# Attention and binary FFN on one core: fp16 halves of q and k taken straight from PSUM, larger pieces in the stores, and a changed use of the PSUM banks

## The chip, the cores and the metric

The kernel runs on one core of one Trainium2 chip. The metric is the device time of one execution in microseconds (us), the median of the runs shown. One further execution was recorded by the hardware profiler; all durations below come from that one. TensorE is PE in the profile (its weight loads PEld), VectorE DVE, ScalarE ACT, GpSimd POOL, SyncE SP. SP only issues DMAs here.

## What is computed

The input x has 16 sequences of 512 rows and 128 features. Each row is normalised once without weights (xn); then two branches read xn, and the output is x plus both:

```
attention:  y = layernorm(xn) * ln_g + ln_b
            q, k, v = y@Wq+bq, y@Wk+bk, y@Wv+bv     16 heads of 8 features
            p = pe@Wp                               pe: a fixed sinusoidal table
            score = (q+u_bias)·k + shift((q+v_bias)·p)    shift: relative positions
            out = softmax(score * 8**-0.5) · v, all heads, @ Wo + bo
FFN:        h = [xn, -xn] @ (+-1 weights k0) * s0;  h = 2 relu(h)      512 wide
            h = h @ (+-1 weights k1) * s1;          h = 2 relu(h)      512 wide
            h = h @ (+-1 weights k2) * s2                              128 wide
```

All inputs are float32, except that the FFN weights are booleans. To use 16-bit matmuls without losing float32 accuracy, the kernel writes a float32 number as a high half and a low half in fp16: hi is the number rounded, lo is the number less hi.

## The kernel before

The work has two stages in one program.

**First stage** (lines 230 to 776). It walks over the 16 sequences. The spine is the FFN: for each sequence `ffn_layer` (L653) does four 128-wide blocks of layer 1 and then four of layer 0 of the next sequence. A block is a group of matmuls (L640) into one PSUM bank, after which ACT writes hi (L617) and DVE writes lo (L618), both from the bank. `ffn_last` (L665) does the third layer into `a_t`, and `ffn_out` (L682) adds it to the residual rows on DVE (L685, L688) and stores them. Into this spine a queue of closures is fed by `more()` (L749), five times a sequence at a fixed rate: `norm` (L308, statistics and scaling on DVE, L318 to L339, with one square root on ACT), `transposed2` (L505, four PE transposes, hi and lo of xn, and the scaled xᵀ that q, k and v use), `project_q` (L543), `project_k` (L563) and `project_v` (L572). When the queue is empty, `more()` issues the stores and the first loads of the second stage (L746).

The projections go through float32 copies: ACT scales and biases the PSUM result into a float32 tile (`scaled`, L522), ACT casts this to hi (L502), and POOL subtracts to get lo (L503), both in `halves_to`:

```
def halves_to(src, hi, lo):
    nc.scalar.copy(hi, src)
    return nc.gpsimd.tensor_tensor(lo, src, hi, ALU.subtract)
```

For q this is done twice: with u_bias for the content scores, and with v_bias for the positions, where two sequences share one tile of 1024 elements a partition. The halves go to scratch tensors in DRAM: each of hi and lo of k, and of q, is stored twice (`K_PARTS`, `Q_PARTS`), since the second stage contracts hi and lo parts stacked over partitions. q for the content is stored as pairs (number, zero) or (zero, number), so the second stage can read two sequences into one block-structured operand; the zeros come from memsets of `qu_b` at the start (L490 to L492). v is stored with one float32 piece of 36 numbers per head and partition.

`ffn_residual` (L658) loads a sequence's x rows once more and adds the output bias on POOL (L662). At the first sequence four are issued at once. `clear_queries` (L494) zeroes pieces of the second stage's query tiles on POOL, one after each `project_k`.

**PSUM.** One pool holds eight banks for the whole kernel: `a_t`, six score tiles `s_t`, and `t_t`. The first stage uses the score tiles and `t_t` as plain banks: three in rotation for the queue's products, four (`F_BANKS`) in rotation for the FFN.

**Second stage** (from L782). For each head 32 units of 16 rows; a unit's scores are matmuls of queries with keys (L797) and with shifted windows of p (L813, L826); DVE takes maxima (L840, L845, L854), PE subtracts them (L859), ACT takes the exponential (L869), and PE multiplies with v (L887). The order on PE, DVE and ACT is written out by hand (`attention_order`); POOL and SP are placed by the framework's planner. In the first stage the planner places all engines, in the program's order as a priority. On the chip every engine's queue runs in order: an instruction that waits holds up all behind it.

Eight units share a block of queries, double-buffered (`load_queries`, L210): 12 DMAs each, four of q for the content (L216) and eight of q for the positions (L220, L224). `load_head` (L196) loads keys (L202), windows and v (L208) for a head, ahead of time. At each head's end `divided` (L939) loads the head's sums (L942) and their reciprocals (L943), multiplies them on POOL (L946) and stores the product (L947).

Of the kernel before, what the change touches and what calls it, by code (L numbers as in the profile page):

```python
# [9 lines left out]
F32 = mybir.dt.float32  # L10
# [10 lines left out]
P = 128  # L21
# [66 lines left out]
def rel_attention_and_binary_ffn(  # L88
# [47 lines left out]
    def scr(name, shape, dt):  # L136
# [4 lines left out]
    qu_scr = scr("qu_scr", [4, DH * H, B, S, 2], F16)  # L141
    qv_scr = scr("qv_scr", [4, DH * H, 5, NL, NC, UL, B], F16)
    k_scr = scr("k_scr", [4, DH * H, B, S], F16)
    p_scr = scr("p_scr", [4, DH * H, 2, WIN + 4], F16)
    pd_scr = scr("pd_scr", [4, DH * H, 2, 2, WIND + 1], F16)
    v_scr = scr("v_scr", [P, H, B, NC * VW], F32)
# [5 lines left out]
    Q_PARTS, K_PARTS = ((0, 2), (1, 3)), ((0, 1), (2, 3))  # L152
# [23 lines left out]
    ps = ctx.enter_context(tc.tile_pool(name="ps", bufs=1, space=bass.MemoryType.PSUM))  # L176
    e_t = [None, early.tile([P, B, NC, NC, 64], F32, tag="e_1", name="e_1")]

    a_t = ps.tile([P, 2, 2 * P], F32, tag="a", name="a_t")

    s_t = [
        [ps.tile([P, 2, NC, 4, B], F32, tag=f"s_{n}_{m}", name=f"s_{n}_{m}") for m in range(2)]
        for n in range(3)
    ]
    t_t = ps.tile([P, 4, 2, P], BF16, tag="t", name="t_t")

    a_flat = a_t.rearrange("p g i -> p (g i)")
    p_banks = [t.rearrange("p c a b r -> p (c a b r)") for ts in s_t for t in ts]
    p_banks.append(t_t.rearrange("p n f i -> p (n f i)").bitcast(F32))
    F_BANKS = (3, 4, 5, 6)  # L190
    t_bank = p_banks[6].rearrange("p (g i) -> p g i", g=2)
# [4 lines left out]
    def load_head(h):  # L196
        m = h % 2
        src = p_scr.rearrange("t (d h) s j -> (t d) h s j", h=H)[:, h]
        src_d = pd_scr.rearrange("t (d h) s n j -> (t d) h s n j", h=H)[:, h]
        for n in range(4):  # L200
            rows_n = slice(32 * n, 32 * n + 32)
            nc.sync.dma_start(  # L202
                k_t[m][rows_n], k_scr.rearrange("t (d h) b j -> (t d) h b j", h=H)[:, h, n::4, :]
            )
            nc.sync.dma_start(win[m][rows_n], src[:, :, 3 - n : 3 - n + WIN])
            r, side = n // 2, n % 2
            nc.sync.dma_start(win_d[m][rows_n], src_d[:, side, :, 1 - r : 1 - r + WIND])
        nc.sync.dma_start(v_t[m], v_scr[:, h].rearrange("p b f -> p (b f)"))  # L208

    def load_queries(h, l):  # L210
        m = l % 2
        qv = qv_scr.rearrange("t (d h) r l a u b -> (t d) h r l (a u b)", h=H)[:, h, :, l]
        qu = qu_scr.rearrange("t (d h) b i m -> (t d) h b (i m)", h=H)[:, h]
        for n in range(4):
            rows_n = slice(32 * n, 32 * n + 32)
            nc.sync.dma_start(  # L216
                qc_t[m][rows_n, :, n // 2].rearrange("p g i m -> p g (i m)"),
                qu[:, n::4, 2 * l * P : 2 * (l + 1) * P],
            )
            nc.sync.dma_start(  # L220
                qp_t[m][rows_n, :, n].rearrange("p s a u b -> p s (a u b)"), qv[:, n : n + 2]
            )
            r, side = n // 2, n % 2
            nc.sync.dma_start(  # L224
                qd_t[m][rows_n, :, r].rearrange("p t a u b -> p t (a u b)"),
                qv[:, r + side : r + side + 3 : 2],
            )


    with ExitStack() as pre:  # L230
        setup = pre.enter_context(tc.tile_pool(name="setup", bufs=1))
        work = pre.enter_context(tc.tile_pool(name="work", bufs=2))
        turns = {}

        def psw(name, banks=(0, 1, 2)):
            turns[banks] = turns.get(banks, 0) + 1
            return p_banks[banks[turns[banks] % len(banks)]]
# [13 lines left out]
        XB = 4  # L251
# [132 lines left out]
        def vectors():  # L384

            for n in range(2):
                nc.gpsimd.tensor_copy(of_feature(rows_d[:, n]), by_feature(rows[:, n]))
            for dst, src in ((wp_d, wp_sb), (wq_d, wq_sb), (wk_d, wk_sb)):
                before = nc.gpsimd.tensor_copy(of_feature(dst), by_feature(src))
            with tc.issue_after(before.ins):  # L390
                clear()
            pt = psw("ptr_rows")
            for n in range(2):
                nc.tensor.transpose(pt[:, 4 * n : 4 * n + 4], rows_d[:, n], ident[:4, :4])
            nc.tensor.transpose(pt[:, 8:10], gb, ident[:2, :2])
            nc.vector.tensor_copy(cols, pt[:, :10])
# [8 lines left out]
        k_mul = pw[:, 1:2]  # L405
        q_mul = sts("q_mul", [P, 1])
# [15 lines left out]
        def powers():  # L422
# [22 lines left out]
            nc.vector.tensor_scalar(q_mul, pw[:, 0:1], scale, None, ALU.mult)  # L445
            nc.vector.tensor_tensor(e_scale, bmax[:, 0:1], bmax[:, 1:2], ALU.mult)
            nc.vector.tensor_scalar(e_scale, e_scale, 2.0 ** -26, None, ALU.mult)
# [7 lines left out]
        def positions():  # L455
            pp = psw("pp")
            nc.tensor.matmul(pp, lhsT=wp_d, rhs=pe_sb, start=True, stop=True)
            p32 = work.tile([P, S], F32, tag="t32", name="p32", bufs=2)
            nc.scalar.activation(p32, pp, AF.Identity, scale=k_mul)
            halves_to(p32, *[t[:, PAD : PAD + S] for t in p_half])  # L460

        def windows():
            for n in range(2):
                for part in K_PARTS[n]:
                    for side, x0, d0 in ((0, PAD, PAD + S - P + 2), (1, 0, PAD - P + 1)):
                        nc.sync.dma_start(p_scr[part, :, side], p_half[n][:, x0 : x0 + WIN + 4])
                        for t in range(2):
                            nc.sync.dma_start(
                                pd_scr[part, :, side, t], p_half[n][:, d0 - 2 * t : d0 - 2 * t + WIND + 1]
                            )  # L470
# [14 lines left out]
        def clear():  # L485
            for t in v_b:
                nc.gpsimd.memset(t, 1.0)
            for t in p_half:
                nc.gpsimd.memset(t, 0.0)
            for ts in qu_b:  # L490
                for t in ts:
                    nc.gpsimd.memset(t, 0.0)  # L492
# [8 lines left out]
        def halves_to(src, hi, lo):  # L501
            nc.scalar.copy(hi, src)  # L502
            return nc.gpsimd.tensor_tensor(lo, src, hi, ALU.subtract)  # L503
# [18 lines left out]
        def scaled(b, n, src, dst):  # L522

            mul = k_mul if n == 2 else q_mul
            if n < 2:
                src = src.rearrange("p (a l m) -> p l a m", a=NC, l=NL)
                dst = dst.rearrange("p (l a m) -> p l a m", l=NL, a=NC)
            nc.scalar.activation(dst, src, AF.Identity, bias=b_cols[:, n : n + 1], scale=mul)

        def t32(b, n):  # L530
            return work.tile([P, S], F32, tag="t32", name=f"t32_{b}_{n}", bufs=2)

        def stored(b, t, dst, parts):
            hv = [work.tile([P, S], F16, tag=f"hv{m}", name=f"hv{m}_{b}", bufs=2) for m in range(2)]
            last = halves_to(t, *hv)
            for m in range(2):
                for part in parts[m]:
                    nc.sync.dma_start(dst[part, :, b, :], hv[m])
            return last

        two = {}

        def project_q(b):  # L543
            pq = psw(f"pq_{b}")
            nc.tensor.matmul(pq, lhsT=wq_d, rhs=x2T[b], start=True, stop=True)
            n = b % 2

            if n == 0:
                two[0] = work.tile([P, S, 2], F32, tag="two", name=f"two_{b}", bufs=1)
            tu = t32(b, 0)  # L550
            scaled(b, 0, pq, tu)
            scaled(b, 1, pq, two[0][:, :, n])
            halves_to(tu, *[t[:, :, n] for t in qu_b[n]])
            for m in range(2):
                for part in Q_PARTS[m]:
                    nc.sync.dma_start(qu_scr[part, :, b], qu_b[n][m])
            if n == 1:
                halves_to(
                    two[0].rearrange("p (q r) n -> p r q n", r=4),
                    *[q[:, :, :, b - 1 : b + 1] for q in qv_all],  # L560
                )

        def project_k(b):  # L563
            pk = psw(f"pk_{b}")
            nc.tensor.matmul(pk, lhsT=wk_d, rhs=x2T[b], start=True, stop=True)
            t = t32(b, 2)
            scaled(b, 2, pk, t)
            last = stored(b, t, k_scr, K_PARTS)
            with tc.issue_after(last.ins):
                clear_queries(b)  # L570

        def project_v(b):  # L572
# [14 lines left out]
            nc.sync.dma_start(v_scr[:, :, b, :], vb.rearrange("p h c w -> p h (c w)"))  # L587
# [21 lines left out]
        acts = {}  # L609
# [4 lines left out]
        def split(src, hi, lo, relu):  # L614

            if relu:
                nc.scalar.activation(hi, src, AF.Relu)  # L617
                nc.vector.scalar_tensor_tensor(lo, src, 0.0, hi, ALU.max, ALU.subtract)  # L618
# [29 lines left out]
        def ffn_split(b, layer, f, ph):  # L648
            part = parts(b, layer + 1, f)
            split(ph, *part, relu=True)  # L650
# [7 lines left out]
        def ffn_residual(b):  # L658
# [3 lines left out]
            nc.gpsimd.tensor_tensor(rows_of, rows_of, bo_sb.unsqueeze(1).to_broadcast([P, NC, D]), ALU.add)  # L662
# [71 lines left out]
        for b in range(B):  # L734
            queue.append(lambda b=b: project_q(b))
# [28 lines left out]
        for b in range(LAST):  # L764
# [6 lines left out]
            for n in range(RB + 1 if b == 0 else 1):  # L771
                if b + n + (RB if b else 0) < B:
                    ffn_residual(b + n + (RB if b else 0))
# [8 lines left out]
    with ExitStack() as att:  # L782
        manual = ExitStack()
# [363 lines left out]
```

## Time and profile before

| what | value |
|---|---|
| median of 3 runs | 1376.68 us (1376.38 to 1377.88) |
| the profiled execution's own time | 1373.51 us |
| its span, first to last instruction | 1371.7 us |
| mean granted TensorE clock | 0.985 |
| busy PE | 1295.0 us (94%) |
| busy DVE | 1137.7 us (83%) |
| busy ACT | 832.6 us (61%) |
| busy POOL | 130.8 us (10%), 115 instructions |
| first score matmul (L797) | 266.5 us after the start |
| DMA traffic | 160.22 MB, of which 58.80 MB by 290 us |

The page gives for each engine the busy tenths in 40 equal slices of the span, some 34 us each. A row of a group reads: line, engine, operation, tiles, shapes, count; durations are given as min/median/max in ns. A row of an order in time reads: start, length, engine, line, operation, and in square brackets the idle time before it with what ended it. PE's ends are modelled, so a PE that is always busy may still have small waits inside.

### The profile page before, as it was taken

The page shows a single profiled execution, that of the slowest core. Times are in us where ns is not written, and L with a number is a line of the kernel's source. Part 1 is how long each engine was busy: PE and PEld are TensorE (multiplying, and loading weights), DVE is VectorE, ACT ScalarE, POOL GpSimd, SP SyncE. Part 2 cuts the span into 40 slices and gives each one's busy share as a digit, 9 for nine tenths or more (in the row PEclk, how much of TensorE's full clock was granted, in tenths as well). Part 3 has the DMA queues.
Part 4 walks back from the last instruction along what each step waited for, and adds up shares of the span by engine and source line. Part 5 has one row for each costly group of instructions (what it writes and reads, how often), then busy time and mean ns, then how long its engine had stood idle before and what let it go on. Part 6 is the DMA issues. An engine that isn't in the chain of part 4 may idle for free. (4 is left out here: it accounts for less than half of the span.)

```text
span 1371.7 us, 55178 instructions
## 1 busy us (share of the span) xinstructions
PE 1295.0 (94%) x23061; PEld 970.3 (71%) x23061; DVE 1137.7 (83%) x2723; ACT 832.6 (61%) x1456; POOL 130.8 (10%) x115
## 2 busy tenths in 40 slices
PE   4988889999999999999999999999999999999966
PEld 2555555577778777777877877778777777777744
DVE  8988754688888888888888888888888888888846
ACT  4566668466666666666666666666666666566630
POOL 4333345010000000000000000000000000000011
PEclk9999999999999999999999999999999999999988
DMA  4587869873232333333333323333333253323288
GB/s 117 171 222 192 191 171 257 242 220 92 76 99 74 94 79 95 95 86 86 93 89 83 94 74 97 83 93 84 95 80 99 75 128 84 95 74 88 68 146 190
DMA packets 243606, 160.22 MB, mean 117 GB/s; under 512 B 79510, under 2 KB 227100, under 8 KB 243356
## 3 DMA queue, kind: packets, MB, share of 16 engines
q1 hardware_dynamic: 243356, 156.69, 43.5%
q8 instruction: 181, 2.97, 0.9%
q14 instruction: 69, 0.57, 0.1%
HBM read 96.34 MB, written 59.48 MB: 114 GB/s over the span
## 5 line engine op out<-in xcount | busy, mean ns | idle before, releaser
L869 ACT ACTIVATE e<-s,e_scale 128x512 f32<-128x512 f32 x1024 | 623.7, 690 | 218.2 <-PE s L859 218.1
L845 DVE TENSOR_TENSOR m<-s,m 128x256 bf16<-128x256 f32 x1024 | 431.6, 422 | 112.9 <-PE s L826 77.6
L797 PE MATMUL s<-q,k 128*128 128x64 f16 x8192 | 406.7, 193 | 2.1 <-issue 1.0
L859 PE MATMUL s<-ident_b,nm 128*128 128x256 bf16 x2048 | 383.8, 275 | 7.3 <-DVE nm L854 7.3
L797 PEld LDWEIGHTS <-k 128*128 128x128 f16 x8192 | 358.5, 98 | 23.6 <-issue 2.8
L840 DVE TENSOR_REDUCE m<-s 128x256 bf16<-128x512 f32 x512 | 348.2, 680 | 1.0 <-ACT e L869 0.6
L813 PE MATMUL s<-q,win 128*128 128x128 f16 (+1 forms) x4096 | 342.8, 206 | 0.1
L887 PE MATMUL a_t<-e,v 128*9 128x256 f32 x4032 | 266.0, 381 | 0.6 <-ACT e L869 0.6
L813 PEld LDWEIGHTS <-win 128*128 128x128 f16 x4096 | 231.4, 98 | 0.3 <-issue 0.3
L826 PE MATMUL s<-q,win_d 128*128 128x64 f16 x2048 | 227.7, 193 | 0.0
L854 DVE TENSOR_REDUCE nm<-t_t 128x2 bf16<-128x256 bf16 x512 | 214.7, 419 | 7.1 <-PE t_t L850 2.9
L859 PEld LDWEIGHTS <-nm 128*128 128x128 bf16 x2048 | 131.0, 98 | 117.8 <-DVE m L845 99.0
L896 ACT COPY av<-a_t 128x256 f32<-128x256 f32 x126 | 46.9, 372 | 186.2 <-PE a_t L887 161.2
L887 PEld LDWEIGHTS a_t<-e,v 128*9 128x9 f32 x4032 | 86.4, 90 | 81.2 <-issue 1.6
L850 PE MATMUL t_t<-ident_b,m 128*128 128x128 bf16 x1024 | 141.3, 220 | 1.4 <-DVE m L845 1.3
L826 PEld LDWEIGHTS <-win_d 128*128 128x128 f16 x2048 | 129.8, 98 | 0.0
L946 POOL TENSOR_TENSOR raw<-raw,rden 128x512 f32<-128x512 f32 x15 | 19.1, 1273 | 992.3 <-DMA rden<-rden_scr 992.3
L640 PEld LDWEIGHTS <-e 128*128 128x128 f16 x512 | 49.6, 98 | 59.7 <-issue 12.6
L850 PEld LDWEIGHTS <-m 128*128 128x128 bf16 x1024 | 80.9, 98 | 11.3 <-DVE m L845 4.9
L618 DVE SCALAR_TENSOR_TENSOR h2l<-s,h2h 128x512 f16<-128x512 f32 x45 | 30.9, 686 | 37.6 <-ACT h2h L617 37.4
L640 PE MATMUL s<-h1l,e 128*128 128x512 f16 x180 | 47.2, 379 | 0.5 <-DVE h1l L618 0.4
L640 PE MATMUL s<-h1h,e 128*128 128x512 f16 x180 | 47.2, 384 | 0.3 <-DVE h1l L618 0.2
(176 smaller groups left out, 888.3 us busy)
## 6 DMA issues: line engine op xcount, KB each, us to landing
q<-qv_scr SPq DMA_DIRECT2D x512, 64.0 KB
q<-qu_scr SPq DMA_DIRECT2D x256, 64.0 KB
qu_scr<-k SPq DMA_DIRECT2D x32, 256.0 KB
k_scr<-hv SPq DMA_DIRECT2D x64, 128.0 KB
qu_scr<-win SPq DMA_DIRECT2D x32, 256.0 KB
qv_scr<-e SPq DMA_DIRECT2D x16, 512.0 KB
k<-k_scr SPq DMA_DIRECT2D x64, 128.0 KB
win<-p_scr SPq DMA_DIRECT2D x64, 79.5 KB
```

Of the source, the lines that this page charges most:

```text
L640: nc.tensor.matmul(ph, lhsT=w[:, t, f * P : (f + 1) * P], rhs=h[t][m], start=(m == 0 and t == 0), stop=(m == 1 and t == n - 1),)
L797: nc.tensor.matmul(sp[:, c % 2, :, :, 4 * g : 4 * g + 4].rearrange("p a r (n m) -> p n (a r) m", m=2), lhsT=kt[:, g, c * P : (c + 1) * P], ...
L813: nc.tensor.matmul(blocks[:, x0 : x0 + (NC + 1) * (len(cs) - 1) + 1 : NC + 1], lhsT=win[h % 2][:, side, y0 : y0 + P], rhs=qp[:, side, :, c ...
L826: nc.tensor.matmul(blocks[:, x0 : x0 + NC + 2 : NC + 1, 2 * t : 2 * t + 2], lhsT=win_d[h % 2][:, t, UP_OFF - 4 * u : WIND - 4 * u], rhs=qd ...
L840: nc.vector.tensor_reduce(st["m"], flat(st["ps"][0]).rearrange("p c x -> p x c"), AX.X, ALU.max)
L845: nc.vector.tensor_tensor(st["m"], flat(st["ps"][1])[:, c], st["m"], ALU.max)
L850: nc.tensor.transpose(st["pt"][:, f, :], st["m"][:, f * P : (f + 1) * P], ident_b)
L854: nc.vector.tensor_reduce(st["nm"], st["pt"], AX.X, ALU.max, negate=True)
L859: nc.tensor.matmul(flat(st["ps"][half])[:, :, f * P : (f + 1) * P], lhsT=st["nm"][:, f : f + 1].to_broadcast([P, P]), rhs=ident_b.unsqueez ...
L869: nc.scalar.activation(st["eT"][:, :, cs, :, i0 : i0 + 4].rearrange("p b c a r -> p (c a) b r"), st["ps"][half].rearrange("p c a r b -> p ...
L887: nc.tensor.matmul(bank[32 * r : 32 * r + VW, g], lhsT=v_t[h % 2][:, v0 : v0 + VW], rhs=pair["eT"][:, b, c], start=(c == 0 and (g == 0 or ...
L896: nc.scalar.copy(pair[half][:, g], bank[:, g])
```

## The change

- `project_q` takes two sequences at a time into two dedicated banks (`q_banks`). `halves_to` is new: ACT writes hi with the bias from PSUM, DVE writes lo from PSUM (`scalar_tensor_tensor`: PSUM plus bias less hi). The four residues of the position queries are four DVE instructions. The float32 copies `t32` and `two`, and `scaled`, are gone. So is POOL's part.
- `k_mul` and `q_mul` go into the weights (three more DVE operations in `powers`), and the softmax scale into `e_scale`.
- q for the content is stored for two sequences at once as a true pair (half the bytes); on loading, POOL zeroes the number that isn't wanted (four memsets of 32 partitions x 512 elements per `load_queries`). The memsets of `qu_b` are gone.
- hi and lo of k are stored once instead of twice and loaded with two DMAs per group instead of one.
- v is stored in one piece of 2304 bytes a partition and sequence, and loaded per head in pieces of 144 bytes.
- PSUM: `a_t` has a pool of its own; the first stage has `q_banks` (two), two rotating banks for the queue, three for the FFN; the second stage opens its own pool for `s_t` and `t_t` after it.
- Residuals: two at the first sequence, then one a sequence ahead of its use (before: four, then three ahead). `clear_queries` follows the residuals of sequences 2 to 9, two memsets each.
- `XB`, the number of x tiles, goes from 4 to 6; k's halves have three buffers instead of two; the copy of `cols` is issued after the first FFN sequence's splits.

```diff
-    qu_scr = scr("qu_scr", [4, DH * H, B, S, 2], F16)
+    qu_scr = scr("qu_scr", [4, DH * H, B // 2, S, 2], F16)
-    k_scr = scr("k_scr", [4, DH * H, B, S], F16)
+    k_scr = scr("k_scr", [2, DH * H, B, S], F16)
-    v_scr = scr("v_scr", [P, H, B, NC * VW], F32)
+    v_scr = scr("v_scr", [P, B, H, NC * VW], F32)
...
+    Q_PARTS, P_PARTS, K_PARTS = ((0, 3), (1, 2)), ((0, 2), (1, 3)), ((0,), (1,))
...
-            nc.sync.dma_start(
-                k_t[m][rows_n], k_scr.rearrange("t (d h) b j -> (t d) h b j", h=H)[:, h, n::4, :]
-            )
+            for x in range(2):
+                nc.sync.dma_start(
+                    k_t[m][32 * n + 16 * x : 32 * n + 16 * x + 16],
+                    k_scr.rearrange("t (d h) b j -> (t d) h b j", h=H)[:, h, n::4, :],
+                )
...
-        nc.sync.dma_start(v_t[m], v_scr[:, h].rearrange("p b f -> p (b f)"))
+        nc.sync.dma_start(v_t[m].rearrange("p (b f) -> p b f", b=B), v_scr[:, :, h])
...
-                qu[:, n::4, 2 * l * P : 2 * (l + 1) * P],
+                qu[:, n // 2 :: 2, 2 * l * P : 2 * (l + 1) * P],
             )
+            nc.gpsimd.memset(qc_t[m][rows_n, :, n // 2, :, 1 - n % 2], 0.0)
...
+        q_banks = psp.tile([P, 2, S], F32, tag="q", name="q_banks")
+        p_banks = [psp.tile([P, S], F32, tag=f"p_{n}", name=f"p_{n}") for n in range(5)]
+        F_BANKS = (2, 3, 4)
-        def psw(name, banks=(0, 1, 2)):
+        def psw(name, banks=(0, 1)):
...
-            nc.vector.tensor_scalar(q_mul, pw[:, 0:1], scale, None, ALU.mult)
+            for t, mul in ((wp_d, k_mul), (wq_d, q_mul), (wk_d, k_mul)):
+                nc.vector.tensor_scalar(t, t, mul, None, ALU.mult)
...
-            for ts in qu_b:
-                for t in ts:
-                    nc.gpsimd.memset(t, 0.0)
...
-        def halves_to(src, hi, lo):
-            nc.scalar.copy(hi, src)
-            return nc.gpsimd.tensor_tensor(lo, src, hi, ALU.subtract)
+        def halves_to(src, n, hi, lo):
+            nc.scalar.activation(hi, src, AF.Identity, bias=b_cols[:, n : n + 1])
+            for r in range(4) if len(src.shape) == 4 else [slice(None)]:
+                nc.vector.scalar_tensor_tensor(
+                    lo[:, r], src[:, r], b_cols[:, n : n + 1], hi[:, r], ALU.add, ALU.subtract
+                )
...
+            for n in range(2):
+                nc.tensor.matmul(
+                    q_banks[:, n],
+                    lhsT=wq_d,
+                    rhs=x2T[b + n].rearrange("p (a l m) -> p l a m", a=NC, l=NL),
+                    start=True,
+                    stop=True,
+                )
+            qu = qu_b[b // 2 % 2]
+            halves_to(q_banks.rearrange("p n j -> p j n"), 0, *qu)
...
+            halves_to(
+                q_banks.rearrange("p n (q r) -> p r q n", r=4), 1, *[q[:, :, :, b : b + 2] for q in qv_all]
+            )
...
-            nc.gpsimd.tensor_tensor(rows_of, rows_of, bo_sb.unsqueeze(1).to_broadcast([P, NC, D]), ALU.add)
+            last = nc.gpsimd.tensor_tensor(
+                rows_of, rows_of, bo_sb.unsqueeze(1).to_broadcast([P, NC, D]), ALU.add
+            )
+            if 2 <= b < 10:
+                with tc.issue_after(last.ins):
+                    for n in range(2):
+                        clear_queries(2 * (b - 2) + n)
...
-            for n in range(RB + 1 if b == 0 else 1):
-                if b + n + (RB if b else 0) < B:
-                    ffn_residual(b + n + (RB if b else 0))
+            for n in range(2 if b == 0 else 1):
+                if b + n + (1 if b else 0) < B:
+                    ffn_residual(b + n + (1 if b else 0))
```

## The prediction

> **What bounds the kernel now.** I read the slices of the page first, then the busy time by stretch, then the order in time of each engine.
>
> ```profile
> PE   4988889999999999999999999999999999999966
> DVE  8988754688888888888888888888888888888846
> POOL 4333345010000000000000000000000000000011
> ```
>
> There are two stages. Up to slice 8 POOL works and PE is below 9; from 266.5 us on, where the first score matmul (L797) starts, PE is full. The change edits the first stage and the loads of the second.
>
> ```profile
> 40.00:180.00 140.00, 121.79 (x707) 70.83 (x707) 118.09 (x385) 90.83 (x162) 54.11 (x44) 0.95 0.77 201
> 180.00:266.00 86.00, 84.72 (x554) 49.81 (x554) 43.78 (x84) 61.15 (x103) 29.61 (x24) 0.98 0.84 231
> ```
>
> Columns after the length: busy PE, weight load, DVE, ACT, POOL, granted clock, DMA share, GB/s. Where DVE is 84% loaded, PE is 87% busy and the clock 0.95; where DVE is 51% loaded, PE is 98.5% busy. So PE bounds the late part, and DVE keeps PE waiting in the early part. The order in time (115 to 124 us) says how:
>
> ```profile
> 115.03 2.91 POOL L503 TENSOR_TENSOR e<-two,e 128x1024 f16<-128x1024 f32 x1
> 116.46 1.51 DVE L330 TENSOR_TENSOR step<-var,root 128x8 f32<-128x8 f32 x1
> 117.91 1.26 POOL L662 TENSOR_TENSOR sums<-sums,bo_sb 128x512 f32<-128x512 f32 x1
> 118.00 1.20 DVE L331 TENSOR_TENSOR step<-step,root 128x8 f32<-128x8 f32 x1
> 119.14 1.15 POOL L503 TENSOR_TENSOR hv<-t,hv 128x512 f16<-128x512 f32 x1
> 119.23 1.54 DVE L332 TENSOR_SCALAR step<-step 128x8 f32<-128x8 f32 x1
> 124.03 1.01 PE L640 MATMUL s<-sums,w_sb 128*128 128x512 f16 x2 [3.92 <-DVE h2l L618]
> ```
>
> Each eight-column norm step of DVE ends when the POOL instruction above it ends; then PE stands for 3.92 us. These two rows, one of an operation on SBUF alone and one that reads PSUM, tell who is held up:
>
> ```profile
> L332 DVE TENSOR_SCALAR step<-step x16: 164/172/3332, 7.6 to 175.3; 128x8 f32<-128x8 f32 x16
> L618 DVE SCALAR_TENSOR_TENSOR h2l<-s,h2h x45: 654/690/693, 24.1 to 261.9; 128x512 f16<-128x512 f32 x45
> ```
>
> The first stretches from 172 ns to 3332, the second never. Mean less median, times the count, over L335, L332, L685, L325, L330, L331, L326 is 7.7+7.3+6.8+4.4+3.9+3.0+2.6 = 36 us of stalled DVE.
>
> **PE's need in the first stage.** L688 ends an FFN sequence every 10.3 us in the tail (244.7, 255.0, 265.3), where PE is full: 15.3 of them are 158 us. On PE's order in time q, k, v and a transposition take 0.86+0.86+0.88+0.43 = 3.0 us a sequence, 16 times 48; with the set-up, 208. The stage runs from the first FFN matmul, 13.6, to 266.5: 253 us, PE at 82%. The missing 45 are idle gaps (2.92 at 17.5 us, 4.38 at 34, then 19.3 in thirteen gaps, nearly all released by DVE lo halves), slow clock behind them (four 10 us stretches at 0.83 and one at 0.66 are 10 us), and smaller pieces.
>
> **The change, part by part.**
>
> Lo halves from POOL to DVE. POOL loses 16 x 1.156 + 8 x 1.27 + 8 x 1.28 + 8 x 2.90 = 62 us and the 3.66 us memsets of qu_b, in whose shadow L332 stood from 13.34 to 16.67. DVE gains, per pair of sequences: two k halves at 0.69 (L618's shape); one of 1024 elements, 1.13 (from L688's 0.341 at 128 and L618's 0.68 at 512, continued); four of 256, about 0.45 each between the same rows: 4.3, times 8 pairs 34.5 us. They read PSUM, so by L618 POOL can't hold them up. POOL keeps 16 residuals of 1.27 and 16 memsets of 0.52, 29 us; before, 103 busy us of POOL cost 36 of DVE, so 10 remain. DVE has 185 busy us in the stage: 185-36+34.5+10 = 194, against PE's 208. The work is traded, not removed; what goes are the blocks of 1.2 to 3.3 us ahead of the FFN's lo halves. Next late would be DVE in the norm part.
>
> The Trainium skill ("SBUF — State Buffer", Who interferes with whom) says that a DVE instruction with at most one SBUF input and no two-port mode never contends with GpSimd; L618's maximum agrees. It also says that a tensor_tensor with two SBUF inputs contends only with GpSimd reads, so that the 16 memsets would stall tensor_scalars alone; by that the remaining stall would be nearer 7 than 10 us.
>
> ACT loses three scalings (0.777, 0.777, 0.808) and casts from SBUF, and has one pass per half: 69 us become 28. ACT was 65% loaded; this shortens ACT's part of each chain, and I count it with the 90% below.
>
> Residuals: four in a row (27.18, 4.93 us) and a fifth (32.07) stood over the 4.38 gap; now two at first. The clears of q_t follow a residual, so POOL is busy 2.3 us at a time in eight sequences: in the 10 above.
>
> I take PE at 90% of the stage, between the 87% and 98.5% of the two stretches, DVE being 194/231 = 84% loaded without long blocks: 208/0.90 = 231, **22 us saved**. Ends: 82% as now (0), and 96% (36).
>
> PSUM. The FFN has three banks instead of four: layer 0 of a sequence issues four 0.43 us groups at once, and the third now waits for an eviction of 1.3 us, of which 0.86 is covered: 0.45 a sequence, 7 us if always, 0 where queue matmuls stand by; I take 1.5. Two banks for k, v and transposes carry three tiles a sequence instead of four on three; q's own pair is held some 6 us of 28: nothing, unless evictions lag, which is the 82% end. The banks change pools at 266.5: at worst the first scores wait for the last FFN eviction (267.35 + 0.69), 1.5 us; I take 1.
>
> Weights times k_mul, q_mul: three more 128x128 DVE operations (about 0.3 us each, L420) less one of 0.15, once: under 1 us, hidden by FFN matmuls; if not, 1.
>
> Stores: 64 fewer issues of 0.43 us on SP, 12.6 MB of 58.8 less, v in 2304-byte pieces instead of 144. DMA is 77% to 84% busy, but little waits for it (6.7 us, L318): nothing taken.
>
> **Second stage.** PE is full, so only new waits count. Its DVE operations read PSUM and never stretch (L845 361/424/426 beside fifteen L946 of 1.27 us): the 256 POOL memsets cost DVE nothing but for L929 (0.24 us). The weak spot is SP at each head's start:
>
> ```profile
> 577.15 0.60 SPq L931 DMA_DIRECT2D rden_scr<-den  x1
> 578.32 0.45 SPq L207 DMA_DIRECT2D win_d<-pd_scr  x1
> 578.82 0.43 SPq L208 DMA_DIRECT2D v<-v_scr  x1
> 579.57 0.62 SPq L943 DMA_DIRECT2D rden<-rden_scr  x1
> ...
> 586.01 0.34 SPq L947 DMA_DIRECT2D head_scr<-raw  x1
> ...
> 591.03 0.43 SPq L224 DMA_DIRECT2D q<-qv_scr  x1
> ```
>
> SP stands from 581.6 to 586.0 for POOL's multiply, which waits for rden; nine query loads stand behind. The last is issued at 591.46, the first score with it starts at 595.95. This 4.5 us comes back at nearly every head's start, against 8 to 11 at other blocks: these starts wait for the landing. Blocks last 16.15 us, those of head starts 16.2 to 18.8; the excess adds to 11.4 us. Whatever delays rden here delays PE, 15 times.
>
> The v load, just ahead, becomes 2048 pieces of 144 bytes. The trace's DMA records show today's v stores with such pieces spread over 1.9 to 2.2 us when undisturbed, today's v loads over 1.0 to 1.5: +0.7 us. The four more k issues (0.43) a head fall in SP's gaps before; if all came here, +1.7. The memset of the last quarter (0.5 us, as L492's 941 ns for twice the elements) follows a load issued 1.8 us before the last: hidden, if POOL isn't waiting for rden; otherwise up to +0.9. Ends: -11.4 (another order frees the starts) to +50 (3.3 x 15); I take 0.4 x 15 = 6, near the v row, as some starts have slack.
>
> The Trainium skill ("DMA: Bandwidth & Descriptors", Specifications) speaks against this piece: under 512 bytes a transfer falls off line rate. Were 144 bytes as dear as 512 (27 ns in the records against 14), the load would take 3.5 us, +2.3, and 15 starts 34 us: the change would lose. The records of 144-byte stores don't show that; loads of that size no row shows.
>
> **Sum.** The execution profiled took 1373.5 (span 1371.7). -22 +1.5 +1 +6 = -13.5: 1360. The median of the runs is 3.2 higher, 1376.7; so **1363**.
>
> **Rivals.**
> - PE-bound stage (0.20): 96%, and head starts no worse: 36 less 1, 1342 (1334 to 1352). For it: 180 to 266 us. Against: DVE's 194.
> - DVE becomes the bound (0.14): the halves fill what the stalls leave, 40 to 180 us holds 118-26+22+6 = 120 busy us again, and the stage gives 6 to 8 less 5: about 1374 (1371 to 1379). A change that doesn't do what it says ends here too: clears behind residuals stall DVE as the halves did.
> - Slower (0.18): the head-start queue. Rden late by v's small reads and by k issues ahead of it, SP late with nine query loads, PE waiting 15 times. From 19.5/15 = 1.3 us a start it outweighs the first stage; at 2.2 us it gives +13.5, 1390.
>
> The forecast has 0.48 (1352 to 1371). Differences under 0.2% (2.7 us) can't be told from none. Faster: 0.48+0.20+0.08; same 0.06; slower 0.18. The range 1338 to 1382 takes in most of the second case and the near edge of the last.
>
> **What will show it.** L332, L335 and L685 near their medians, and gaps before L640 under 1 us; the clock near 1.0 over 40 to 180; first L797 near 246; DVE above 80% until then. In the second stage: blocks of 16.15 us against the head starts' 16.2 to 18.8, and the gap before head_scr<-raw on SP. I am wrong if L332 still stretches, if PE waits for q's or k's PSUM banks, or if head starts exceed 17.5 us.

## The result, and the profile after

After the change the kernel takes **1437.68 us** (median of 4 runs, 1436.83 to 1438.57); the kernel before, run beside it, 1376.53 (1372.17 to 1377.88). The ratio is 1.0444 [1.0415, 1.0472]: slower, where 1363 (1338 to 1382) was forecast. The profiled execution took 1437.72 us, span 1435.9, mean granted clock 0.959 (before 0.985).

The slices of the page come first, since they show that two opposite things happened:

```profile
PE   6999998999898989898989899989898989898976
DVE  8999765888787878786878787878787868687846
POOL 3111001211111111111111111111111111111111
```

The first slices of PE are fuller than before. But from slice 10 on, where PE read 9 everywhere, almost every other slice is now an 8: one dent for each pair of slices. A slice is 35.9 us and a head lasts about 70, so the dent comes once a head.

The first score matmul moved from 266.5 to 241.4 us: the first stage gained **25 us**. From there to the end it took 1105.2 us before and 1194.5 after: the second stage lost **89 us**.

**First stage.** The stretch from 40 to 180 us, by busy PE, weight load, DVE, ACT, POOL, granted clock, DMA share, GB/s:

```profile
40.00:180.00 140.00, 133.67 (x844) 78.14 (x842) 127.35 (x425) 84.49 (x147) 15.73 (x20) 1.00 0.49 158
```

PE went from 121.79 to 133.67, the clock from 0.95 to 1.00, POOL from 54.11 to 15.73. The norm step that stretched to 3332 ns (L332 before, L330 now) and the FFN's lo halves (L618 before, L596 now), by min/median/max:

```profile
L330 DVE TENSOR_SCALAR step<-step x16: 135/162/529, 7.3 to 144.1; 128x8 f32<-128x8 f32 x16
L596 DVE SCALAR_TENSOR_TENSOR h2l<-p,h2h x60: 669/691/693, 20.4 to 234.8; 128x512 f16<-128x512 f32 x60
```

The step is hardly held any more (529 ns at most); the operation that reads PSUM is as it was. Over all of DVE's groups up to the first score, mean less median, times the count, adds to 38 us before and 15 after.

**Second stage.** The order in time of SP at the end of a head, start and length of each issue:

```profile
573.80 0.62 SPq L938 DMA_DIRECT2D rden<-rden_scr  x1
574.46 0.46 SPq L199 DMA_DIRECT2D win_d<-pd_scr  x1
574.96 0.43 SPq L193 DMA_DIRECT2D k<-k_scr  x1
579.53 0.34 SPq L942 DMA_DIRECT2D head_scr<-raw  x1
579.91 0.43 SPq L193 DMA_DIRECT2D k<-k_scr  x1
580.39 0.43 SPq L197 DMA_DIRECT2D win<-p_scr  x1
580.87 0.43 SPq L199 DMA_DIRECT2D win_d<-pd_scr  x1
581.40 0.56 SPq L200 DMA_DIRECT2D v<-v_scr  x1
582.06 1.37 SPq L208 DMA_DIRECT2D q<-qu_scr  x1
...
589.69 0.42 SPq L217 DMA_DIRECT2D q<-qv_scr  x1
590.22 0.59 SPq L916 DMA_DIRECT2D den<-av  x1
```

As before, SP stands some 4 us (575.4 to 579.5) for POOL's multiply. But now all twelve query loads are behind this, and four pieces of `load_head` between; before, two pieces of it (`win_d`, `v`) and three query loads had been issued ahead and nine were behind. The issue to watch is the last, `den<-av`: it goes out at 590.22, behind everything. This is so at every head: the store goes out ahead of all twelve query loads at 14 of 14 starts (before: at one of 14, and ahead of nine at the others), and `den<-av` goes out 16.6 us after the first score of the block that ends there (median; before: 12.3). DVE and PE at that place:

```profile
587.27 0.68 DVE L835 TENSOR_REDUCE m<-s 128x256 bf16<-128x512 f32 x1
592.09 0.25 DVE L924 RECIPROCAL den<-den 128x16 f32<-128x16 f32 x1 [4.14 <-DMA den<-av]
593.01 0.61 PE L854 MATMUL s<-ident_b,nm 128*128 128x256 bf16 x2 [3.71 <-DVE nm L849]
```

The reciprocal of the sums stands in DVE's order written out by hand, between the maxima of the scores. It waits 4.14 us for a small DMA; every maximum behind it waits too, and PE, which needs the maxima, stands 3.71 us. The same place by stretches (busy PE, clock, DMA share, GB/s) shows a second bill:

```profile
587.00:591.00 4.00, 2.31 (x51) 1.00 0.48 135
591.00:595.00 4.00, 1.99 (x21) 0.60 0.15 28
595.00:599.00 4.00, 4.00 (x59) 0.54 0.34 99
```

PE stands from 589.3 to 593.0. In the second and third stretch the mean granted clock is 0.60 and 0.54: PE starts again slowly, and the block that follows is longer too. Over 300 to 1300 us, the waits of that reciprocal and of PE (total, times, longest), before and then after:

```profile
DVE den L929 <- DMA den<-av: 10.5, 12, 2.6
PE s L859 <- DVE nm L854: 7.2, 9, 2.2
```

```profile
DVE den L924 <- DMA den<-av: 64.8, 13, 7.0
PE s L854 <- DVE nm L849: 59.5, 13, 6.5
```

To sum it up, I took the length of each block of eight units above 16.15 us. The fifteen blocks that end at a head's start exceed it by 10.2 us in all before and by 80.4 after; the fifteen behind them by 2.2 and 17.9; the very first block of the stage lasts 17.4 and 20.2. The differences, 70.2, 15.7 and 2.8, make 88.7 of the 89 us. The 70.2 and 15.7 are the two bills together. PE's standing for the maxima grew by 52 us (7.2 to 59.5). And the trace's record of the clock has 13 stretches at 0.50 between 300 and 1310 us, 6.8 us long but for the first, where before it has none; PE's busy time inside them, halved, is 31 us of lost work (an estimate from this record). Together these are 83 of the 86 us. So more than a third of the loss was paid in clock.

### The profile page after: what moved, and what is told of

It is laid out like the page before. It is cut to its first block, busy times and chain, and to the rows that moved or that the text cites. A ratio compares the mean times of both kernels' runs of the same rounds, so it can differ in the third digit from the quotient of the medians.

```text
span 1435.9 us, 55680 instructions
## 1 busy us (share of the span) xinstructions
PE 1318.8 (92%) x23061; PEld 990.2 (69%) x23061; DVE 1147.0 (80%) x2782; ACT 805.8 (56%) x1399; POOL 236.7 (16%) x326
## 5 line engine op out<-in xcount | busy, mean ns | idle before, releaser
L840 DVE TENSOR_TENSOR m<-s,m 128x256 bf16<-128x256 f32 x1024 | 431.2, 421 | 129.1 <-PE s L821 92.0
L854 PE MATMUL s<-ident_b,nm 128*128 128x256 bf16 x2048 | 397.4, 283 | 64.5 <-DVE nm L849 64.5
L792 PE MATMUL s<-q,k 128*128 128x64 f16 x8192 | 418.3, 196 | 2.3 <-DVE e L596 1.7
L792 PEld LDWEIGHTS <-k 128*128 128x128 f16 x8192 | 372.0, 100 | 27.7 <-issue 3.2
L808 PE MATMUL s<-q,win 128*128 128x128 f16 (+1 forms) x4096 | 350.4, 209 | 0.8 <-issue 0.8
L212 POOL MEMSET q<- 32x512 f16 x256 | 171.7, 671 | 783.6 <-DMA q<-qu_scr 695.4
L808 PEld LDWEIGHTS <-win 128*128 128x128 f16 x4096 | 238.7, 100 | 0.9 <-issue 0.9
L618 PEld LDWEIGHTS <-e 128*128 128x128 f16 x512 | 49.6, 98 | 60.1 <-issue 12.6
L924 DVE RECIPROCAL den<-den 128x16 f32<-128x16 f32 x62 | 15.2, 245 | 84.8 <-DMA den<-av 69.0
L595 ACT ACTIVATE h2h<-p 128x512 f16<-128x512 f32 x60 | 35.9, 598 | 51.5 <-PE p L618 51.3
L618 PE MATMUL p<-h1h,e 128*128 128x512 f16 x240 | 62.7, 382 | 0.0
```

Of the source, the lines that this page charges most:

```text
L212: nc.gpsimd.memset(qc_t[m][rows_n, :, n // 2, :, 1 - n % 2], 0.0)
L618: nc.tensor.matmul(ph, lhsT=w[:, t, f * P : (f + 1) * P], rhs=h[t][m], start=(m == 0 and t == 0), stop=(m == 1 and t == n - 1),)
L792: nc.tensor.matmul(sp[:, c % 2, :, :, 4 * g : 4 * g + 4].rearrange("p a r (n m) -> p n (a r) m", m=2), lhsT=kt[:, g, c * P : (c + 1) * P], ...
L808: nc.tensor.matmul(blocks[:, x0 : x0 + (NC + 1) * (len(cs) - 1) + 1 : NC + 1], lhsT=win[h % 2][:, side, y0 : y0 + P], rhs=qp[:, side, :, c ...
L840: nc.vector.tensor_tensor(st["m"], flat(st["ps"][1])[:, c], st["m"], ALU.max)
L854: nc.tensor.matmul(flat(st["ps"][half])[:, :, f * P : (f + 1) * P], lhsT=st["nm"][:, f : f + 1].to_broadcast([P, P]), rhs=ident_b.unsqueez ...
```

## The experiments

The theory after this comparison: **SP's order**. The second k issue per group (four more a head) makes the planner place `load_head`, the store that waits for POOL, and the queries differently, so `den<-av` goes out late. The rivals: **v's pieces** of 144 bytes delay the chain of `rden`; the **memsets** on POOL delay the multiply, and so the store. For the first stage: **POOL holds DVE**, against fewer passes on ACT. A last group tries to mend the order. "Excess" is that of the fifteen blocks that end at a head's start, "den" the reciprocal's wait over 300 to 1300 us. The median is of all executions; the columns behind the ratio are of the one that was profiled.

| kernel | median us | ratio to before [95%] | first score | rest of the span | first block | excess | den |
|---|---|---|---|---|---|---|---|
| before | 1376.53 |  | 266.5 | 1105.2 | 17.4 | 10.2 | 10.5 |
| after | 1437.68 | 1.0444 [1.0415, 1.0472] | 241.4 | 1194.5 | 20.2 | 80.4 | 64.8 |
| b_k8 | 1432.54 | 1.043 [1.0377, 1.0484] | 269.1 | 1156.4 | 17.4 | 55.5 | 47.5 |
| a_k4 | 1363.97 | 0.9927 [0.9901, 0.9952] | 242.3 | 1122.1 | 21.2 | 23.5 | 22.3 |
| a_poolstore | 1359.91 | 0.9902 [0.9875, 0.9929] | 241.3 | 1116.8 | 22.5 | 15.8 | 14.1 |
| a_early | 1486.68 | 1.0827 [1.0777, 1.0877] | 241.2 | 1240.4 | 21.1 | 0.9 | 0.3 |
| a_early2 | 1360.07 | 0.9891 [0.9861, 0.9921] | 241.2 | 1115.9 | 20.1 | 1.5 | 19.4 |
| a_k4_nomemset | 1359.85 | 0.9891 [0.9861, 0.992] | 239.9 | 1117.4 | 20.0 | 18.3 | 19.0 |
| a_k4_v | 1352.75 | 0.983 [0.9801, 0.9859] | 241.7 | 1111.5 | 21.1 | 10.2 | 7.3 |
| a_k4_pool | 1393.35 | 1.0133 [1.0102, 1.0165] | 266.9 | 1120.8 | 19.7 | 21.5 | 20.3 |
| c_base | 1355.87 | 0.9878 [0.9832, 0.9925] | 240.7 | 1114.2 | 27.5 | 10.3 | 9.1 |
| c_spread | 1359.83 | 0.9911 [0.9873, 0.995] | 242.9 | 1115.1 | 28.2 | 8.8 | 9.4 |
| c_spread_ps | 1351.13 | 0.9835 [0.9799, 0.9872] | 242.4 | 1107.6 | 27.5 | 0.7 | 7.4 |
| c_ps_res2 | 1343.32 | 0.9775 [0.9737, 0.9814] | 241.6 | 1096.1 | 19.1 | 0.8 | 7.8 |

**b_k8** is the kernel before with nothing but k's split load.

```diff
-            nc.sync.dma_start(k_t[m][rows_n], k_scr...[:, h, n::4, :])
+            for x in range(2):
+                nc.sync.dma_start(k_t[m][32*n+16*x : 32*n+16*x+16], k_scr...[16*x : 16*x+16, h, n::4, :])
```

> The kernel before, with one part of the change: each load of keys is split into two loads of 16 partitions (8 issues a head on SP instead of 4, the same bytes). Theory Q (queue order): four more issues a head make the planner put five more of the head's loads, and the store of the divided head that waits for POOL, ahead of all twelve query loads at each head's start; the first stage stays (first score matmul near 266 us) and the second loses what the changed kernel loses, 85 to 90 us: 1460 us. Theory M (the POOL memsets behind the query loads make PE wait) and theory V (the 144-byte pieces of v keep the DMA engines from the queries) both expect no change, 1376 us.

The rest of the span grew by 51 us (85 to 90 were expected), from the same bytes in the same places: four more issues a head are enough. SP's order at a head's start is that of the changed kernel, with four pieces of `load_head` and all twelve query loads behind the store:

```profile
599.09 0.34 SPq L949 DMA_DIRECT2D head_scr<-raw  x1
599.47 0.43 SPq L203 DMA_DIRECT2D k<-k_scr  x1
...
601.42 0.38 SPq L218 DMA_DIRECT2D q<-qu_scr  x1
...
608.33 0.58 SPq L923 DMA_DIRECT2D den<-av  x1
```

And it is the same wait (300 to 1300 us):

```profile
DVE den L931 <- DMA den<-av: 47.5, 13, 5.9
```

**a_k4** is the whole change with k stored twice and loaded with one issue of 32 partitions per group, as before.

```diff
-    K_PARTS = ..., ((0,), (1,))
+    K_PARTS = ..., ((0, 2), (1, 3))
...
```

> The changed kernel with that part undone: hi and lo of k stored twice and loaded with one issue per group, as before. Theory Q: second stage back to 1105 to 1110 us, first scores near 241 to 245, so 1350 to 1360 us. Theories M and V: the memsets and the pieces of v are still there, so near 1437 us.

The kernel is now 0.7% faster than before, and the rest of the span is 72 us shorter than after's. Still it is 17 us longer than before's:

```profile
DVE den L922 <- DMA den<-av: 22.3, 13, 5.1
```

So the split costs 51 us alone, the rest of the change 17, and both together 89: 21 us come only from the meeting of the two. How they meet was not tried.

**a_poolstore** is after with one store on another queue.

```diff
-            nc.sync.dma_start(head_scr[...], raw)
+            nc.gpsimd.dma_start(head_scr[...], raw)
```

> The changed kernel, eight key loads kept; the store of the divided head is issued from POOL's queue behind its multiply, so that SP no longer stands for it. Theory Q, if the standing is what costs: query loads some 4.5 us earlier at each head's start, blocks of 21 us back to about 16.5, so 1365 us (1355 to 1385). If the mere number of issues ahead costs, a few us of gain at most, near 1430. Theories M and V: near 1437.

All eight k loads stay, and the 89 us shrink to 12, 5 of them in the first block. SP at a head's start:

```profile
562.50 2.50 SPq L208 DMA_DIRECT2D q<-qu_scr  x1
...
571.36 0.60 SPq L916 DMA_DIRECT2D den<-av  x1
```

The queries follow `load_head` without the standing of 4 us. Neither the count of issues nor the bytes of k are the price, then; it is what they stand behind.

**a_early** loads the next head two blocks earlier, ahead of the queries for a head's third block instead of those for the next head's first; v is then loaded before the older head's last products have read theirs, so these use another head's v.

```diff
-                    if nl % NL == 0:
-                        load_head(nl // NL)
+                    if nl % NL == 2 and nl // NL + 1 < H:
+                        load_head(nl // NL + 1)
```

> The changed kernel, eight key loads kept; the next head's loads are asked for two query blocks earlier, so that none of them lies between the sums and the queries at a head's start. Theory Q: no block over 17 us, second stage 1100 to 1105 us, 1345 to 1355 us. Theories M and V: near 1437.

The head starts' excess went (0.9 us), but the kernel is the slowest of all: PE's products wait for v's landing, in 300 to 1300 us

```profile
PE a_t L882 <- DMA v<-v_scr: 103.6, 13, 8.7
```

so the buffer that is still read decides how early a load may go. **a_early2** takes all but v early:

```diff
...
+                    if nl % NL == 2 and nl // NL + 1 < H:
+                        load_head(nl // NL + 1, v=False)
                     if nl % NL == 0:
-                        load_head(nl // NL)
+                        load_v(nl // NL)
```

> The changed kernel, eight key loads kept; keys and windows of the next head are asked for two query blocks earlier, v where it was. Theory Q: the blocks that end at a head's start fall from 21 to 23 us to 16.2 to 16.7 with nothing but v's issue between the sums and the queries, no wait for v; second stage 1100 to 1108 us, in all 1343 to 1352 us. If the memsets or the 144-byte pieces of v hold up the queries by themselves, these blocks stay 17 to 18 us and the total is 1355 to 1365.

The head starts are free (1.5 us), and 78 us come back. But the sixteen loads now stand in a bunch (591 to 600 us) before the queries of another block, whose blocks have an excess of 19.0 us, and the reciprocal waits there: the same queue, at another place.

**a_k4_nomemset** is a_k4 without POOL's zeroing in `load_queries`.

> a_k4 without the POOL memsets behind the query loads, so that the numbers that should be zero stay in the queries (this part of the computation is left out). a_k4 had 23.5 us of excess in the blocks that end at a head's start, the kernel before 10.2. If the memsets make the queries late: back to about 10, 1351 us. If v's small pieces do: no change, 1364.

The medians differ by 4.1 us, but the two intervals overlap; the excess falls from 23.5 to 18.3. POOL's multiply starts no earlier without the memsets (6.0 us after the block's first score with them, 6.1 without; medians over the starts). So the memsets' price is small, 4 to 5 us by these two numbers and not clear of the noise, and it does not come by way of the multiply. **a_k4_v** is a_k4 with v stored and loaded as before.

```diff
-    v_scr = scr("v_scr", [P, B, H, NC * VW], F32)
+    v_scr = scr("v_scr", [P, H, B, NC * VW], F32)
...
```

> a_k4 with v stored and loaded as before (144-byte pieces in the store, 2304 bytes in the load). If v's small pieces delay the reciprocals' landing and the queries behind it: excess of the head starts from 23.5 back to about 10, 1351 us, and the first stage perhaps 1 to 3 us later for the slower stores. If the memsets do it: no change, 1364.

It gives 11.2 us, and the head starts' excess falls from 23.5 to 10.2, which is before's: v's small pieces are what a_k4 mainly lost. SP's order is the same in both kernels at 13 of the 15 stores, so here the transfer itself is the cost: with small pieces the last byte of v moves 4.4 us after the load's issue, without 2.9, and POOL's multiply starts 0.8 us later (medians over the heads).

**a_k4_pool** adds work to POOL that nothing waits for, in the first stage alone: in `project_k`, on a 128x512 float32 tile `idle`.

```diff
...
+            for _ in range(3):
+                nc.gpsimd.tensor_tensor(idle, idle, idle, ALU.subtract)
```

> a_k4 with three idle POOL subtractions of 128x512 float32 behind each product of k, some 61 us in all, about what the change took from POOL; nothing waits for them. Theory S (POOL's instructions stall DVE, and that kept PE waiting): eight-column norm steps stretch to 1 to 3 us again, PE idles behind lo halves, and the first score matmul comes at 255 to 265 us instead of 242. If ACT's lighter load or the DMA traffic made the first stage faster: it stays at 242 to 245.

The first score moves from 242.3 to 266.9, where it was before the change. The stretch from 40 to 180 us, a_k4 first, then a_k4_pool:

```profile
40.00:180.00 140.00, 134.02 (x839) 79.00 (x838) 127.22 (x420) 84.10 (x146) 15.75 (x20) 0.99 0.55 180
```

```profile
40.00:180.00 140.00, 125.82 (x739) 72.46 (x737) 132.77 (x429) 73.35 (x128) 48.64 (x54) 0.94 0.49 159
```

POOL has 33 us more; PE has 100 matmuls fewer and its clock is 0.94; ACT does less, not more. The scaling of the norm, the same 64 instructions, in each kernel's first 240 us (count, busy, mean ns):

```profile
L331 DVE TENSOR_SCALAR xn<-xn,st,root 128x128 f32<-128x128 f32 x64 | 24.2, 447 | 0.0
```

```profile
L333 DVE TENSOR_SCALAR xn<-xn,st,root 128x128 f32<-128x128 f32 x64 | 36.0, 608 | 0.1
```

Over all of DVE's groups up to the first score, mean less median, times the count, adds to 17 us in a_k4 and 36 in a_k4_pool, against 38 before the change. PE itself waits for POOL 0.8 us at most in a_k4_pool's first stage. This is what the 25 us were: POOL holding DVE's operations on SBUF.

**c_base** stores k once, with a group's four sequences side by side, loads it with one issue a group (the source read twice), and has v as before.

```diff
...
+            nc.sync.dma_start(k_t[m][rows_n]..., k_scr...[:, h, n].unsqueeze(0).to_broadcast([2, 2*DH, 4*S]))
```

> The changed kernel with v as before, and with k still stored once but loaded with one issue per group (the two copies made by a repeated read). Theory Q: what counts is the number of issues, not that k is stored once; as a_k4_v, 1352 us (1348 to 1357), head starts with 10 us of excess. If the halved store is what harms the second stage: near 1430.

It shows that k's halved store can be had without the issues; against a_k4_v nothing is gained: the excess is the same, and the first block is 6.4 us longer. **c_spread** adds to it: queries first, then the next head's loads in two pairs behind the third and fourth blocks' queries, v last.

```diff
...
+                    load_queries(*loads[nl])
+                    if nl % NL == 0:
+                        load_v(nl // NL)
+                    elif nl % NL > 1 and nl // NL + 1 < H:
+                        load_head(nl // NL + 1, range(2 * (nl % NL) - 4, 2 * (nl % NL) - 2), False)
...
```

> c_base with the next head's loads asked for two groups at a time behind the queries of the head's second and third blocks, and v behind those of the last. Theory Q: no block waits for a load of the head; excess over all blocks under 10 us, 1340 to 1347 us. If the spread loads push the sums and reciprocals back elsewhere, as in a_early2's second block: 1350 or more.

No gain: the rest of the span is 0.9 us longer than c_base's, excess 8.8 against 10.3. With eight of the twelve queries still behind the store, placing the head's loads elsewhere is worth little. **c_spread_ps** moves that store as a_poolstore did:

> c_spread with the store of the divided head issued from POOL's queue. If SP standing for POOL's multiply is still what delays the head starts: their excess goes from what c_spread shows to under 3 us, 2 to 8 us less in all. If c_spread's head starts are free already: no difference.

Now the excess is 0.7 us and the rest of the span 7.5 shorter. What is left late is the first block, 27.5 us, where a residual came late:

```profile
PE a_t L623 <- DVE sums L679: 9.6, 1, 9.6
DVE sums L679 <- POOL sums L647: 7.1, 1, 7.1
```

**c_ps_res2** therefore has residuals two ahead:

```diff
-            for n in range(2 if b == 0 else 1):
-                if b + n + (1 if b else 0) < B:
-                    ffn_residual(b + n + (1 if b else 0))
+            for n in range(3 if b == 0 else 1):
+                if b + n + (2 if b else 0) < B:
+                    ffn_residual(b + n + (2 if b else 0))
```

> c_spread_ps with residuals loaded two sequences ahead of their use instead of one. In the changed kernel the last residual but one comes at 243.7 us, DVE and the leftover FFN matmuls wait for it, and the first block takes 20.2 us where the kernel before took 17.4. If that wait is why: 2 to 4 us less, first block near 17.5. Else no difference.

The first block falls to 19.1 us and the kernel to **1343.32 us, 0.9775 [0.9737, 0.9814]** of before: faster than both kernels. The gain over c_spread_ps, 7.8 us, is more than the 2 to 4 expected from after's wait: the wait of 9.6 us fell to 2.5. PE's slices, to be held against those after the change:

```profile
PE   6989999899999999999999999999999999999966
```

## Why the prediction was wrong

**First stage: right.** 22 us forecast, 25 measured (266.5 to 241.4). DVE has 192.31 us busy from 13 to 242 (194 forecast). PE's need, 208 us as reckoned in the prediction, is 91% of a stage of 228 (90% taken); the 90% was a choice between two stretches, so that it came so near is partly luck. The new lo halves cost 4.67 us a pair (4.3): k 0.743 each, q for the content 1.27, positions four times 0.477. POOL still holds a few steps (up to 1.8 us in L323 and 1.7 in L324, 2.4 in L333; 15 us in all where 10 were forecast, or nearer 7), but PE's gaps from 40 us on stay under 1.4 us. a_k4_pool shows that the mechanism was this one.

**PSUM: near.** The three FFN banks cost gaps of 0.16 us a sequence in the tail (0.45 at most); the first scores wait 1.75 us at the hand-over (1 was taken, 1.5 called the worst).

**Memsets: nearly.** 672 ns each, not 0.5; DVE's maxima (L840) are as before, 360/424/426. By a_k4_nomemset they cost 4 to 5 us, which isn't clear of the noise.

**v's pieces: near.** 0.7 us x 15 = 10.5 was the row's price, 6 was taken for all of the head starts; a_k4_v says 11 to 13. The records show 14 ns a piece of 144 bytes.

The Trainium skill ("DMA: Bandwidth & Descriptors", Specifications) asks for 512 bytes or more for line rate. The records agree on the rate: a piece of 2304 bytes takes 93 ns, 25 bytes a ns, one of 512 takes 27 ns, 19 a ns, and one of 144 takes 14 ns, 10 a ns. But the +2.3 us a head that the prediction weighed for this, with 27 ns for a small piece too, did not come: a_k4_v shows some 0.9.

**Residuals one ahead: not priced.** Only the gap they left was counted. With it, one late residual in front of the first scores cost 8 us in c_spread_ps (first block 27.5, with two ahead 19.1). After's own first block is 2.8 us above before's. Its trace has the same wait: PE stands 3.21 us at 246.20 for the residual addition on DVE (L674), which follows POOL's at 243.72; before has no such wait. No run takes it out of this kernel alone.

**The step that failed** is "The four more k issues (0.43) a head fall in SP's gaps before; if all came here, +1.7". They were priced as lengths to be added, while each issue is also a place in an order that the planner makes anew. b_k8 measures this sentence alone: +51 us of rest, 3.4 a start, without v's pieces or a memset, where +1.7 a start was the worst thought of; with the other parts of the change it is 72 (after against a_k4). The whole second stage, bounded at +50, lost 89. The prediction's own sign of being wrong, head starts over 17.5 us, came true: the blocks that end there last 16.15 + 80.4/15 = 21.5.

Behind it stands a **wrong reading** of the trace of before: "these starts wait for the landing". I saw the last query issued at 591.46 and the first score with it at 595.95, and took the 4.5 us for the landing. The next two rows, one of SP and one of DVE, would have told otherwise:

```profile
591.56 0.58 SPq L921 DMA_DIRECT2D den<-av  x1
```

```profile
593.51 0.25 DVE L929 RECIPROCAL den<-den 128x16 f32<-128x16 f32 x1 [0.37 <-DMA den<-av]
```

Queued right behind the last query is the small load that DVE waits for; those waits (10.5 us) are before's excess of 10 to 11 us. Start by start the excess rises and falls with the wait of the reciprocal (correlation 0.99 before and after), and from 300 us on PE waits for no query load in either trace. That whatever delays rden delays PE 15 times holds, as a_k4_v shows, but by way of `den<-av`. With the wrong waiter, I did not see that DVE stands with it, nor that PE's standing would be paid again in clock.

**The slower rival** (0.18) had the place and half of the mechanism: SP late at the head starts with the queries behind. But it had rden late, by v's reads and k's issues; after the change rden's load goes out 0.5 us before the first score of its block and POOL's multiply starts 4.3 us after it, where before it was 0.2 and 5.3 (medians). What came late is `den<-av`, 4.3 us. Its price was 2.2 us a start, 1390; measured are (70.2 + 15.7)/15 = 5.7 us. That the PE-bound rival's 1342 is near c_ps_res2's 1343 is chance: the first stage gives 25 us there, not 36, and the rest comes from head starts that are better than before's (rest of the span 1096.1 against 1105.2).

That the planner's new order comes from the issues alone is shown by b_k8, and by a_poolstore that what costs is the standing store in that order; by which of its costs the planner chose it was not tried.

## What to carry to other kernels

Before adding an issue to a queue, list what stands in it at the stage's tightest place: who waits for POOL there, which loads are behind, and which small load at the end holds an engine whose order is written out by hand. Four issues of 0.4 us a head cost 3.4 us a head here (b_k8), and after's eight k loads with the store on POOL's queue cost little (a_poolstore): a store that waits for another engine is better issued from that engine's own queue. And an idle time is read by the row that ended it, not by the nearest transfer in time.

## What the runs showed of the hardware

- Where PE stood for 3.7 us (to 593.01) the granted clock was 0.60 and 0.54 in the stretches 591 to 595 and 595 to 599 us, and 1.00 behind them. The fifteen blocks that end at a head's start are 80.4 us too long in all, and the blocks behind them 17.9.
- A small operation of DVE on SBUF (128x4, 0.16 us) was held up to 1.8 us while POOL worked (memsets, at 10.5 us); 512-element operations that read PSUM kept 669 to 693 ns in the same stage.
- A memset of 32x512 float16 with a stride took POOL 672 ns, where the 128x512 float32 one of the first stage took 527.
- An issue on SP, 0.43 us as a rule, takes 1.4 to 2.5 us now and then (1.78 at 584.43 us after the change, 2.50 at 562.50 in a_poolstore). Why, no run shows; the 1.37 at 582.06 us has a release by PE inside it.
